# Weights times V summed in one PSUM bank over a group's eight cells, each product placed inside the scores of a later cell

## The chip, the cores and the metric

The kernel runs on one core of a Trainium2 chip. The time is the device time of the whole program in microseconds (us). A profiled execution adds a trace of every instruction on the engines: PE (TensorE, matmuls), DVE (VectorE), ACT (ScalarE), POOL (GpSimd) and SP, which here only issues DMAs. PEld is PE's loading of weights.

## The reference, cut to what matters

Two transformer blocks follow each other, on x of 2 x 1024 tokens of width 256, with 16 heads of 16. Each block has self attention over the 1024 tokens, cross attention over 64 context rows, and a feed-forward part (eight experts with the best two per token in the first block, a plain one in the second). What the change touches is the self attention of both blocks:

```
scores = einsum('bhqd,bhkd->bhqk', q, k) / sqrt(16)
attn = softmax(scores, axis=-1)
out = einsum('bhqk,bhkd->bhqd', attn, v)
```

All of it is in float32.

## The kernel before, in words

`self_attention` runs once for each block. It cuts its work into 128 cells. A cell is one block of 128 keys for one half of the queries (512) and four heads; eight cells in a row are a group (`h`): they share queries and heads, and go through all 1024 keys. Two batches, two halves of the queries and four sets of heads give 16 groups.

For each cell two kinds of scores are made, four tiles of each, one tile for a head:

- kind "b", keys by queries: two matmuls (the queries are kept as a high and a low part) and a third with one-rows that subtracts each query's maximum. ACT turns the tile into weights with exp (L873), written to `pt`.
- kind "a", queries by keys, for the cell that lies `LEAD` = 10 cells ahead: two matmuls, and DVE takes the maximum of each row (L866, `mx`). At a group's end `collect` (L916 to L918) and `largest` (L770, L772) bring the maxima into the form that the third matmul of kind "b" needs.

`scores` (L878) writes these in **waves**. There are four lanes, one for each head and each on 32 rows of the PE array. Lanes 0 and 1 do "b" and then "a", lanes 2 and 3 the other way round. One wave is one matmul of each lane, so a cell has five waves. A tile takes one of PSUM's eight banks: `bank()` pops the head of the list `free`, and the bank goes back to the tail once its drain (ACT or DVE) is written down. PE must wait where a popped bank is still being read. The wave in which a tile begins is therefore the place of such a wait (L894 is the line of all these matmuls).

`product` (L929) multiplies the weights of cells past with V (L938; V carries a column of ones, so that the sums of the weights come with it). It takes a bank from the list, holds it for one or two cells, copies it with ACT (L947 for the first of a group, to `acc`; L950 for the others, to `part`) and adds the part to `acc` (L951, on POOL while maxima are still made, on DVE after that). It is called after the scores, at each even cell for the two cells before, or at an odd cell for one of them when there is little other work (`alone`).

At the end of each cell the loop (L1030 to L1065) hands out other work: a `Stream` of tasks with costs and due times, which are projections of keys and queries (`project_heads`, L646, with ACT L633 and DVE L634), values (L609), the output projection (L440), transposes and norms (L372), cross attention (L1182, L1216, L1269, L1283) and so on. Each step pops its own bank and gives it back. `owed` and `most` say how much is handed out in one cell. Between the two loops lie the experts, and after the second one the last feed-forward part; what the loops leave over is done there.

Engines work in the order in which the program is written; the order on PE, DVE, ACT and SP is set by hand (`manual_schedule`), and only semaphores stand between them.

Of the kernel before, what the change touches and what calls it, by code (L numbers as in the profile page):

```python
# [41 lines left out]
F32 = mybir.dt.float32  # L42
# [4 lines left out]
ALU = mybir.AluOpType  # L47
# [4 lines left out]
P = 128  # L52
# [4 lines left out]
TB = S // P  # L57
# [11 lines left out]
VW = 18  # L69
# [135 lines left out]
def two_blocks(  # L205
# [16 lines left out]
    nc = tc.nc  # L222
# [6 lines left out]
    )  # L229
    banks = psum.tile([P, 8, 512], F32, tag="banks", name="banks")  # L230
    free = list(range(8))

    def bank():


        i = free.pop(0)
        return i, banks[:, i, :]
# [79 lines left out]
    def helper():  # L317

        return nc.gpsimd if maxima[0] else nc.vector
# [175 lines left out]
    def next_heads():  # L495

        npair[0] += 1
        return npair[0] - 1

    def invert(n, sm):  # L500

        nc.vector.reciprocal(sm, sm)
        nc.sync.dma_start(out=turns[n], in_=sm)
# [22 lines left out]
    def self_attention(layer, tail, heads, arrive, extra, when_ready, beside=None):  # L526
# [6 lines left out]
        names = f"s{layer}"  # L533
        pools = ExitStack()

        def results_pool():
            side = {"side": "right"} if layer else {}
            return tail.enter_context(tc.tile_pool(name=f"opool{layer}", bufs=2, **side))
# [4 lines left out]
        if layer == 0:  # L543
            opool = results_pool()
# [13 lines left out]
        stream, later = Stream(RATE[layer]), {}  # L558
        maxima[0] = True

        def at_cell(cell, go):
            later.setdefault(cell, []).append(go)

        extra(stream, vpool, at_cell)
        ncell = 64 * B
        xT, V, ot, sums, acc = {}, {}, {}, {}, {}
        QB, mx = {}, {}
        exps = {}
# [207 lines left out]
        def finish(h, cell):  # L776


            b, qh, g = h // 8, h // 4 % 2, h % 4
            if g == 0:  # L780
                ot[b, qh] = opool.tile([P, 2, 512], F32, tag="ot", name=f"ot_{names}{b}{qh}")
            if layer == 0 and h >= 8 * B - 2:

                if g == 3:
                    stream.add(
                        side_by_side([acc.pop(h - 1), acc.pop(h)], ot[b, qh][:, 1, :]), 2.0,
                        mark="compact", rank=80,
                    )
                    project(b, qh, ["compact"])
                return  # L790
            if g % 2 == 0:
                sm = small.tile([P, 32], F32, tag="sums", name=f"sums_{names}{h}")
                sums[g // 2] = next_heads(), sm
            n, sm = sums[g // 2]
            dst = ot[b, qh][:, g // 2, :]
            send(acc.pop(h), n, g % 2, sm)
            if g % 2 == 1:
                by = opool.tile([P, 512], F32, tag="by", name=f"by_{names}{h}", bufs=1)
                gather(n, dst)
                at_cell(cell + 1, lambda: invert(n, sm))  # L800
                at_cell(cell + 2, lambda: spread_out(n, by))

                late = 3 + maxima[0]
                at_cell(cell + late, lambda: divide(dst, by))
                if g == 3:
                    at_cell(cell + late + 1, lambda: project(b, qh))
# [68 lines left out]

            return products, drain

        def scores(lanes):  # L878

            lanes = [[score(*t) for t in lane] for lane in lanes]  # L880
            at = [[0, None] for _ in lanes]
            while any(lanes):
                done = []
                for lane, now in zip(lanes, at):
                    if not lane:
                        continue
                    products, drain = lane[0]
                    if now[1] is None:
                        now[1] = bank()
                    i, sc = now[1]  # L890
                    lhsT, rhs = products[now[0]]
                    now[0] += 1
                    last = now[0] == len(products)
                    nc.tensor.matmul(sc, lhsT=lhsT, rhs=rhs, start=now[0] == 1, stop=last)  # L894
                    if last:
                        done.append((drain, i, sc))
                        lane.pop(0)
                        now[:] = 0, None
                for drain, i, sc in done:
                    drain(sc)  # L900
                    free.append(i)

        def early(cell):

# [19 lines left out]
                    break  # L924
                most -= cost

        alone = set()

        def product(cells):  # L929

            h = cells[0] // 8
            b, g = h // 8, h % 4
            for cell in cells:
                stream.until(("values", b, cell % 8 & 6))
            n, o = bank()
            for cell in cells:
                for j in range(4):
                    nc.tensor.matmul(  # L938
                        o[32 * j : 32 * j + VW, :],
                        lhsT=V[b][:, cell % 8, 4 * g + j, :],  # L940
                        rhs=exps.pop((cell, j)),
                        start=(cell == cells[0]),
                        stop=(cell == cells[-1]),
                    )
            if cells[0] % 8 == 0:
                acc[h] = opool.tile([P, 512], F32, tag="acc", name=f"acc_{names}{h}")
                nc.scalar.copy(acc[h], o)  # L947
            else:
                part = opool.tile([P, 512], F32, tag="part", name=f"part_{names}{cells[0]}", bufs=3)
                nc.scalar.copy(part, o)  # L950
                helper().tensor_tensor(acc[h], acc[h], part, ALU.add)  # L951
            free.append(n)
            if cells[-1] % 8 == TB - 1:
                at_cell(cells[-1] + 3, lambda: finish(h, cells[-1] + 3))

        def begin():

# [20 lines left out]
        if layer == 0:  # L978
            ws = twice()
            norm_pairs(0, TB, ln, x_turned(0), f"{names}0", arrive)  # L980
            other_constants()
            prepare()
            for i in range(2):
                spread_bias(i)
            for _ in first_heads(ws):
                pass
            ready_for_exp()
            stream.add(biases(), 3.3, last=6, mark="biases")
        else:
            beside(begin)  # L990
            beginning.close()
            stage[0] = mixture.spare
            opool, qpool = results_pool(), weights_pool()
            stream.made.add(("QB", 0))
        stream.made.update([("norm", 0), ("Q", 0)])
        add_values(0, -99, [("norm", 0)])
        add_heads(2)
# [12 lines left out]
        if layer == 0:  # L1010

            fill_up(-LEAD, 4.0)
            owed = 0.0
            for ahead in range(0, LEAD, 2):
                cell = now[0] = ahead - LEAD
# [13 lines left out]
        owed = 0.0  # L1029
        for cell in range(ncell + 2):  # L1030
            now[0] = cell
            ahead = cell + LEAD
            if ahead < ncell and ahead % 16 == 0:
                need_heads(ahead // 8)
            has_a, has_b = ahead < ncell, cell < ncell
            maxima[0] = has_a
            lanes = []
            for j in range(4):
                tiles = [("b", cell, j)] * has_b + [("a", ahead, j)] * has_a
                lanes.append(tiles[::-1] if j > 1 else tiles)  # L1040
            scores(lanes)
            if ahead % 8 == 7 and has_a:
                h = ahead // 8
                collect(h)
                stream.add(largest(h), 0.75, first=cell + 1, last=cell + 2, mark=("QB", h))
            if (cell + 1) % 8 == 0 and cell + 1 < ncell:
                stream.until(("QB", (cell + 1) // 8))
            for go in later.pop(cell, []):
                go()
            owed = min(owed, 3.0) + max(stream.pace(cell), 0.0 if has_a else 2.0)  # L1050
            if cell >= 2 and cell % 2 == 0:
                product([c for c in (cell - 2, cell - 1) if c not in alone])
                if owed < 2.5:
                    continue
            most = 3.0
            while owed > 0.6 and most > 0.0:
                cost = stream.step(cell)
                if cost is None:
                    break
                owed -= cost  # L1060
                most -= cost

            if cell % 2 == 1 and most > 2.0 and cell < ncell:
                alone.add(cell - 1)
                product([cell - 1])  # L1065
        pools.close()
        return stream, later

# [990 lines left out]
    stream, later, _, _ = block(0, tail)  # L2059
# [41 lines left out]
    def beside(begin):  # L2101

        both = Stream(0.0)
        both.add(begin(), 40.0, mark="begun", rank=50)
        both.add(mixture.run(NFIRST, NEVEN), 72.0, mark="slots")
        both.rest({}, 0)
        ready_for_exp()
        mixture.others()
        slots.close()

    with ExitStack() as tail:
        stream, later, made, ready = block(1, tail, heads, beside)
# [157 lines left out]
```

## Time and profile before

| what | us |
|---|---|
| three runs | 1635.91, 1643.36, 1648.19 |
| median | 1643.36 |
| profiled execution, its own time | 1634.33 |
| its span (first to last instruction) | 1632.5 |
| PE busy | 1510.0 (92%) |
| DVE busy | 1056.7 (65%) |
| ACT busy | 940.5 (58%) |
| POOL busy | 459.6 (28%) |
| L866, maxima on DVE, 1024 of 680 ns | 633.0 |
| L873, exp on ACT, 1024 of 605 ns | 532.6 |
| L938, products on PE, 2048 of 639 ns | 280.9 |
| L951, adds on POOL, 149 of 1283 ns | 191.2 |
| L950, part copies on ACT, 163 of 601 ns | 97.9 |

Busy time is the union of an engine's records, so records that overlap count once. A float32 matmul of the source stands in the trace as two (1024 products are 2048 records). A row of the timeline gives start, duration, engine, line and operation, the tile written and the tiles read, how many follow each other, and in brackets how long the engine had been idle and for whom. A row of the waits view says which engine and line waited for which, in total. A row of the windows view gives each engine's busy time in a stretch, then the granted clock of PE as a share of full speed, the DMA share, and GB/s.

### The profile page before, as it was taken

Reading aid. Unit: us, or ns where it says so; the run is one execution under the profiler, and the core shown is the slowest. Engines: PE = TensorE matmul, PEld = TensorE weight load, DVE = VectorE, ACT = ScalarE, POOL = GpSimd, SP = SyncE. Lnnn points to the kernel's source line nnn. Section 1 sums busy time; section 2 is a strip of 40 time slices with the busy share of each in tenths; the row PEclk is TensorE's granted clock in tenths of the full one; section 3 lists DMA queues with packets and bytes.
Section 4 is the critical chain, followed back from the end, with each engine's and each line's share of the span. In section 5 each row is a group of like instructions: output and inputs, shape, how many; then the busy total and the mean of one; then the engine's idle time right before and its main releaser. Section 6 shows DMA issues by size and latency. Waiting matters only on the chain. (4 is left out here: it accounts for less than half of the span.)

```text
span 1632.5 us, 30066 instructions
## 1 busy us (share of the span) xinstructions
PE 1510.0 (92%) x11230; PEld 885.1 (54%) x11230; DVE 1056.7 (65%) x2287; ACT 940.5 (58%) x1820; POOL 459.6 (28%) x584
## 2 busy tenths in 40 slices
PE   7999998988898986999999998999998998989998
PEld 3534544444444454788888764444444444446766
DVE  6798777887887764531114576978788886855400
ACT  3478777856776752423322336876776786774321
POOL 1234333433533302121112023411353344421010
PEclk9799999999998897999999999999999999999999
DMA  4446331201100120666566123111231112000000
GB/s 162 157 157 243 100 107 48 82 34 47 59 28 14 34 81 33 233 241 209 194 204 241 66 95 100 34 60 41 85 105 47 34 53 76 21 8 21 14 13 26
DMA packets 66481, 147.36 MB, mean 90 GB/s; under 512 B 10650, under 2 KB 24860, under 8 KB 65948
## 3 DMA queue, kind: packets, MB, share of 16 engines
q1 hardware_dynamic: 62876, 135.89, 24.3%
q0 software_dynamic: 3456, 9.51, 1.6%
q8 instruction: 90, 1.47, 0.4%
q14 instruction: 59, 0.48, 0.1%
HBM read 92.61 MB, written 52.51 MB: 89 GB/s over the span
## 5 line engine op out<-in xcount | busy, mean ns | idle before, releaser
L866 DVE TENSOR_REDUCE mx_s<-banks 128x1 f32<-128x512 f32 x1024 | 633.0, 680 | 105.8 <-PE banks L894 103.7
L873 ACT ACTIVATE pt_s<-banks 128x512 f32<-128x512 f32 x1024 | 532.6, 605 | 121.8 <-PE banks L894 117.6
L938 PE MATMUL banks<-pt_s,v_s 128*18 128x512 f32 x2048 | 280.9, 639 | 51.4 <-DVE mx_s L866 50.5
L951 POOL TENSOR_TENSOR acc_s<-acc_s,part_s 128x512 f32<-128x512 f32 x149 | 191.2, 1283 | 345.3 <-ACT part_s L950 343.7
L894 PE MATMUL banks<-qb_s,ones 2*128 2x512 f32 x1024 | 207.9, 407 | 0.0
L950 ACT COPY part_s<-banks 128x512 f32<-128x512 f32 x163 | 97.9, 601 | 79.3 <-PE banks L938 47.2
L1799 PE MATMUL banks<-w_slot,h_s 128*128 128x256 f32 x640 | 143.1, 380 | 0.1
L938 PEld LDWEIGHTS banks<-pt_s,v_s 128*18 128x18 f32 x2048 | 43.4, 99 | 180.6 <-DVE mx_s L866 124.1
L1799 PEld LDWEIGHTS banks<-w_slot,h_s 128*128 128x128 f32 x640 | 120.6, 190 | 18.8 <-DVE mx_s L866 1.3
L1808 DVE SCALAR_TENSOR_TENSOR ys<-banks,gate,b 128x256 f32<-128x256 f32 x40 | 19.3, 483 | 154.8 <-PE banks L1799 152.5
L1814 POOL DMA_INDIRECT results<-ys,to x40 | 38.8, 970 | 246.6 <-DVE ys L1808 178.2
L894 PEld LDWEIGHTS banks<-qb_s,ones 2*128 2x128 f32 x1024 | 101.2, 194 | 7.7 <-DVE qb_s L772 0.3
L1775 ACT ACTIVATE h_s<-banks,w_slot 128x256 f32<-128x256 f32 x104 | 43.6, 470 | 105.5 <-issue 64.9
L1769 PE MATMUL banks<-xsT,w_slot 128*128 128x256 f32 x416 | 94.8, 381 | 0.7 <-ACT xsT L379 0.7
L1769 PEld LDWEIGHTS banks<-xsT,w_slot 128*128 128x128 f32 x416 | 77.5, 190 | 12.6 <-ACT xsT L379 1.4
L1932 ACT ACTIVATE h_f<-banks,w_ff 128x512 f32<-128x512 f32 x32 | 22.0, 687 | 73.9 <-PE banks L1929 73.9
L1775 ACT ACTIVATE h_s<-banks,spare 128x256 f32<-128x256 f32 x56 | 23.5, 470 | 61.3 <-issue 30.4
L1237 POOL TENSOR_TENSOR sc_c<-sc_c,mx_c 128x512 f32<-128x512 f32 x36 | 37.6, 1045 | 73.2 <-DVE mx_c L1236 73.1
L1941 PE MATMUL banks<-w_ff,h_f 128*128 128x256 f32 x256 | 57.3, 380 | 0.0
L1929 PE MATMUL banks<-hT_f,w_ff 128*128 128x512 f32 x128 | 56.4, 593 | 0.0
L1216 PE MATMUL banks<-kbd,q_c 32*128 32x128 f32 x512 | 48.5, 293 | 4.5 <-DVE mx_s L866 2.9
L1941 PEld LDWEIGHTS banks<-w_ff,h_f 128*128 128x128 f32 x256 | 48.0, 190 | 7.8 <-issue 1.4
(362 smaller groups left out, 3216.2 us busy)
## 6 DMA issues: line engine op xcount, KB each, us to landing
w_slot<-in_ff_w_dram SPq DMA_DIRECT2D x40, 576.0 KB
sorted_rows<-fill SPq DMA_DIRECT2D x36, 520.0 KB
w_slot<-in_ff_w_dram SPq DMA_DIRECT2D x26, 514.0 KB
whole<-acc_s SPq DMA_DIRECT2D x30, 256.0 KB
spare<-in_ff_w_dram SPq DMA_DIRECT2D x14, 514.0 KB
q_parts<-spare SPq DMA_DIRECT2D x14, 512.0 KB
k_parts<-spare SPq DMA_DIRECT2D x12, 512.0 KB
KS<-k_parts SPq DMA_DIRECT2D x12, 512.0 KB
```

The lines of the kernel that those rows point to most:

```text
L866: return products, lambda sc: nc.vector.tensor_reduce(to, sc, AX.X, ALU.max)
L873: nc.scalar.activation(pt, sc, AF.Exp, scale=SCALE)
L894: nc.tensor.matmul(sc, lhsT=lhsT, rhs=rhs, start=now[0] == 1, stop=last)
L938: nc.tensor.matmul(o[32 * j : 32 * j + VW, :], lhsT=V[b][:, cell % 8, 4 * g + j, :], rhs=exps.pop((cell, j)), start=(cell == cells[0]), st ...
L950: nc.scalar.copy(part, o)
L951: helper().tensor_tensor(acc[h], acc[h], part, ALU.add)
L1216: nc.tensor.matmul(p[:, t * P : (t + 1) * P], lhsT=q[rows, g, t * P : (t + 1) * P], rhs=kbd[rows, g, b].rearrange("p u k -> p (u k)"), sta ...
L1769: nc.tensor.matmul(ph[:, n, :], lhsT=w[:, at : at + P], rhs=xT[:, k, :], start=(k == 0), stop=(k == 1),)
L1775: nc.scalar.activation(h1[:, f, :], ph[:, n, :], AF.Gelu, bias=w[:, W_B1 + f : W_B1 + f + 1])
L1799: nc.tensor.matmul(py, lhsT=h1[:, f, h * P : (h + 1) * P], rhs=w[:, f * D : (f + 1) * D], start=(f == 0), stop=(f == 7),)
L1929: nc.tensor.matmul(ph, lhsT=w1[:, at : at + P], rhs=hT[:, k, :], start=(k == 0), stop=(k == 1))
L1941: nc.tensor.matmul(py[:, n, :], lhsT=h1[:, f, t * P : (t + 1) * P], rhs=w2[:, f * D : (f + 1) * D], start=(f == 0), stop=(f == 7),)
```

## The change

Bank 7 (`SUMS`) is taken out of the list for the length of each loop, and seven banks remain in turn. `product` now does one cell. It adds into bank 7 over all eight cells of a group: the first starts the sum, the eighth ends it, and one ACT copy takes it to `acc`. The parts and their adds are gone. `scores` calls `product(cell - 2)` between its third wave and its fourth. Banks that the scores have emptied no longer go back one by one: those of the first three waves go back together after the third, and those of the last two at the end, taken alternately from the two halves. The rules of how much other work a cell gets lose the case of even cells, and `most` falls from 3.0 to 1.8.

```diff
+    SUMS = 7
...
-        def scores(lanes):
+        def scores(lanes, beside=None):
             lanes = [[score(*t) for t in lane] for lane in lanes]
             at = [[0, None] for _ in lanes]
+            emptied, wave = [], 0
             while any(lanes):
...
                 for drain, i, sc in done:
                     drain(sc)
-                    free.append(i)
+                emptied.extend(i for _, i, _ in done)
+                wave += 1
+                if wave == 3 or not any(lanes):
+                    half = (len(emptied) + 1) // 2
+                    for n in range(half):
+                        free.extend(emptied[n::half])
+                    emptied = []
+                if wave == 3 and beside:
+                    beside()
...
-        def product(cells):
+        def product(cell):
+            h, n = divmod(cell, 8)
             b, g = h // 8, h % 4
-            for cell in cells:
-                stream.until(("values", b, cell % 8 & 6))
-            n, o = bank()
-            for cell in cells:
-                for j in range(4):
-                    nc.tensor.matmul(
-                        o[32 * j : 32 * j + VW, :],
-                        lhsT=V[b][:, cell % 8, 4 * g + j, :],
-                        rhs=exps.pop((cell, j)),
-                        start=(cell == cells[0]),
-                        stop=(cell == cells[-1]),
-                    )
-            if cells[0] % 8 == 0:
+            stream.until(("values", b, n & 6))
+            o = banks[:, SUMS, :]
+            for j in range(4):
+                nc.tensor.matmul(
+                    o[32 * j : 32 * j + VW, :],
+                    lhsT=V[b][:, n, 4 * g + j, :],
+                    rhs=exps.pop((cell, j)),
+                    start=(n == 0),
+                    stop=(n == TB - 1),
+                )
+            if n == TB - 1:
                 acc[h] = opool.tile([P, 512], F32, tag="acc", name=f"acc_{names}{h}")
                 nc.scalar.copy(acc[h], o)
-            else:
-                part = opool.tile([P, 512], F32, tag="part", name=f"part_{names}{cells[0]}", bufs=3)
-                nc.scalar.copy(part, o)
-                helper().tensor_tensor(acc[h], acc[h], part, ALU.add)
-            free.append(n)
-            if cells[-1] % 8 == TB - 1:
-                at_cell(cells[-1] + 3, lambda: finish(h, cells[-1] + 3))
+                at_cell(cell + 3, lambda: finish(h, cell + 3))
...
+        free.remove(SUMS)
...
-            scores(lanes)
+            if has_b:
+                scores(lanes, (lambda: product(cell - 2)) if cell >= 2 else None)
+            else:
+                product(cell - 2)
...
-            if cell >= 2 and cell % 2 == 0:
-                product([c for c in (cell - 2, cell - 1) if c not in alone])
-                if owed < 2.5:
-                    continue
-            most = 3.0
+            most = 1.8
             while owed > 0.6 and most > 0.0:
...
-            if cell % 2 == 1 and most > 2.0 and cell < ncell:
-                alone.add(cell - 1)
-                product([cell - 1])
+        free.append(SUMS)
```

More of the change, by code (lines that the diff above doesn't have):

```diff
@@ L925, in fill_up @@
                 most -= cost
-        alone = set()
-        def product(cells):
-            h = cells[0] // 8
+        def product(cell):
+            h, n = divmod(cell, 8)
             b, g = h // 8, h % 4
-            for cell in cells:
-                stream.until(("values", b, cell % 8 & 6))
-            n, o = bank()
-            for cell in cells:
-                for j in range(4):
-                    nc.tensor.matmul(
-                        o[32 * j : 32 * j + VW, :],
-                        lhsT=V[b][:, cell % 8, 4 * g + j, :],
-                        rhs=exps.pop((cell, j)),
-                        start=(cell == cells[0]),
-                        stop=(cell == cells[-1]),
-                    )
-            if cells[0] % 8 == 0:
+            stream.until(("values", b, n & 6))
[9 more added lines that the diff above has]
+            if n == TB - 1:
                 acc[h] = opool.tile([P, 512], F32, tag="acc", name=f"acc_{names}{h}")
                 nc.scalar.copy(acc[h], o)
-            else:
-                part = opool.tile([P, 512], F32, tag="part", name=f"part_{names}{cells[0]}", bufs=3)
-                nc.scalar.copy(part, o)
-                helper().tensor_tensor(acc[h], acc[h], part, ALU.add)
-            free.append(n)
-            if cells[-1] % 8 == TB - 1:
-                at_cell(cells[-1] + 3, lambda: finish(h, cells[-1] + 3))
+                at_cell(cell + 3, lambda: finish(h, cell + 3))
         def begin():
```

## Prediction

> **What bounds the kernel now.** I read the busy shares first, then the windows of the two attention loops, then the waits, then one stretch of the timeline.
>
> The page says PE 92%. That share is inflated, because a matmul's record lasts longer than the array needs it (0.39 to 0.49 us for one that frees the array after 0.23). What tells more is the pair of windows over the two loops of 128 cells each:
>
> ```profile
> core 0: us, PE busy (x) PEld busy (x) DVE busy (x) ACT busy (x) POOL busy (x), PEclk, DMA share, GB/s
> 47.50:574.80 527.30, 482.67 (x4166) 233.93 (x4166) 425.37 (x840) 380.20 (x736) 197.56 (x249) 0.94 0.25 86
> 964.40:1468.80 504.40, 464.27 (x4138) 223.50 (x4140) 387.06 (x722) 371.15 (x710) 182.00 (x210) 0.96 0.18 60
> ```
>
> The loops take 527.3 + 504.4 = 1031.7 us, or 4.06 us a cell for 254 cells (the first of each counts to the start). DVE works 3.2 us of that and ACT 3.0. No engine is full: the cell is a chain between engines. The waits name its links:
>
> ```profile
> engine line waited for: us in total, times, longest us
> POOL acc_s L951 <- ACT part_s L950: 343.7, 89, 17.3
> ...
> PEld banks L894 <- DVE mx_s L866: 137.4, 235, 1.7
> PEld banks L938 <- DVE mx_s L866: 124.1, 174, 4.2
> ...
> PE banks L938 <- DVE mx_s L866: 50.5, 66, 3.8
> ```
>
> Scores (L894) and products (L938) wait for DVE's maxima (L866), since each needs a bank that DVE is still reading. POOL waits for its parts, so its adds are off the path. The timeline shows one cell that has no other work:
>
> ```profile
> 128.51 1.05 PE L938 MATMUL banks<-pt_s,v_s 128*18 128x512 f32 x8
> ...
> 129.50 0.50 PE L894 MATMUL banks<-QS02h,KS 32*128 32x512 f32 x2
> ...
> 129.83 0.40 PE L894 MATMUL banks<-QS02l,KS 32*128 32x512 f32 x2
> ...
> 130.06 0.39 PE L894 MATMUL banks<-qb_s,ones 2*128 2x512 f32 x2
> ...
> 130.87 0.40 PE L894 MATMUL banks<-qb_s,ones 2*128 2x512 f32 x2
> ...
> 131.20 0.62 PE L938 MATMUL banks<-pt_s,v_s 128*18 128x512 f32 x4
> ```
>
> Starts, read downward: product, 0.99 us to the first wave of scores, 0.33 to the second, 0.23 to the third, 0.81 to the fifth, 0.33 to the next product. The period is 2.69. DVE's four reductions take 2.47 in a row (1132.79, x4), 0.60 from one to the next, each 0.68 until its bank is free. So DVE is nearly full in this cell. The product lies just where PE would else wait: the fifth wave's maximum needs 0.39 (matmul) + 0.04 + 0.68 (L866) + 0.05 (release to PE) = 1.16 us until its bank is free, and the product fills 0.33 + 0.98 = 1.31 of that.
>
> By this pattern a cell costs max(2.65, 2.44 + s) us, s being PE time of other tasks at its end; 0.10 of it is the switch to such a task and is paid only where there is one. Over the 254 cells that gives 903 us. The real 1032 hold 129 us of excess: products that stall for a DVE bank, DVE stretched by POOL's adds, and half clock after the stalls.
>
> **What goes.** 163 part copies on ACT (97.9 us) and 163 adds (149 on POOL, 191.2 us; 14 on DVE). Neither engine bounds a cell, so this alone saves only what the adds do to DVE:
>
> ```profile
> 110.67 1.28 POOL L951 TENSOR_TENSOR acc_s<-acc_s,part_s 128x512 f32<-128x512 f32 x1 [1.63 <-ACT part_s L950]
> 110.77 1.22 DVE L917 CAST spread<-top_s 128x16 fp32r<-128x16 f32 x1
> ...
> 113.40 1.19 PE L938 MATMUL banks<-pt_s,v_s 128*18 128x512 f32 x8 [1.86 <-DVE mx_s L866]
> ```
>
> The cast takes 0.18 us elsewhere and 1.22 beside the add; behind it the maxima come late, and the product waits 1.86 us. Summed over the loops, DVE rows that outlast their usual time lose 20 us. The product's bank wait goes too: bank 7 is its own. What is late next is the score wave, below.
>
> **What moves.** I read the order of the new program: first three waves, product, last two waves, then the other tasks. With seven banks, the fourth score of wave one waits for DVE, and so does the fourth of wave three, the second of wave four and the second of wave one. The product itself waits for nothing. Following the free list by hand: wave one's fourth score takes the bank of the previous cell's third maximum (call it a0), wave three's fourth takes that of the last maximum (a1), wave four's second takes this cell's first.
>
> Chain of a cell without other work, from the start of a0's reduction: a1 starts at 0.60, ends at 1.28, PE is released at 1.33 (wave one's release at 0.73, plus 0.34 and 0.25 for two waves, gives 1.32, the same). Product at 1.66. Wave four at 1.66 + 0.98 = 2.64. Its bank is free since 1.20 + 0.68 = 1.88, so no wait. Wave five at 2.97, done at 3.36, next a0 at 3.40 to 3.41. **The period is 3.41 instead of 2.65.** The product now stands on the chain, and the 1.16 us behind wave five, which it used to fill, are open for other tasks: up to 0.84 us of them cost nothing. A cell with more is bound by PE: 0.33 + 0.23 + 0.33 + 0.98 + 0.33 + 0.33 = 2.57 with the switch, plus s.
>
> The order lists what follows each cell. Priced by PE blocks of the trace (one projection of heads L646 1.8 us, L609 and half of L440 1.8, L770 0.5, a block of L1216 1.7, L1269 0.9, plus 0.1 for each visit), 141 of 254 cells have at most 0.84 us, 104 of them nothing; 113 have more, 245 us together.
>
> - 141 x 3.41 = 481
> - 113 x 2.57 + 245 = 536
> - sum 1017, against 1032 measured before
>
> So the new ideal is nearly the old reality. What decides is how much excess comes on top. DVE has 3.41 - 2.47 = 0.9 us free in a plain cell, which hides most of its small work (0.6 of statistics, 0.65 of collecting), and the product stalls are gone, so I expect far less than 129:
> - 23 projections of heads: DVE's second half (L634) starts after PE and ACT (0.69) and ends some 1.75 us after the block; the maximum behind it frees its bank at 2.5, wave four wanted it at 1.9: 0.6 each, 14 us
> - two banks taken by small tasks: wave one waits for a1, 0.57 each, some 7 cells: 4 us
> - clock (next part): 20 us
> - the 3 us wait of the second layer's keys for a DMA, and DVE lumps over 0.9: 12 us
>
> Together 50. The copy of the finished sum (32 of 0.6 us on ACT) must end before the next group's first product, more than 2 us later: nothing, and if that cover failed, 0.6 each, 19 us. The sending of a finished sum (`finish`) stays three cells behind its last cell; that cell's product now comes half a cell later and its add no longer follows, so SP's stores find it ready as before. Other tasks take at most 1.8 us a cell instead of 3.0; by the order 7.6 us of PE work (258.6 against 251.0) moves behind the loops, where PE is full (40.00 of 40.00 us in the last whole slices): +8. No DMA is added; those of finish, keys and queries keep their cells, give or take one.
>
> Sum: 1017 + 50 + 8 - 1032 = **+43 us**. Bounds: excess 0 gives -7, the old 129 gives +122.
>
> **A rule against the row.** The Trainium skill, TensorEngine Tiling (Array Packing), Key Properties, says that changing the tiling mode drains the array. Scores use four row tiles, products four column tiles, so each product inside the scores is two changes more wherever other tasks follow. By the row a change costs about 0.1 us: 0.33 against 0.23 from wave to product, 0.98 for a product alone against 0.92 in a pair (1.84 to the next start for x16). By the rule taken at its word, each side exposes the whole tail of a matmul, 0.39 in place of 0.1; the plain cell would be 3.41 + 0.58 = 4.0 and the kernel 150 us slower. I take the row, as the same two changes stand in it; it already speaks against the change by 0.2 a cell.
>
> The page TensorE: Matmul & The Clock Gate, Part 1, says that the clock halves after an idle window of about 3.4 us. Here it halves sooner:
>
> ```profile
> 114.20:117.60 3.40, 3.40 (x28) 2.22 (x24) 2.83 (x7) 0.88 (x2) 1.27 (x1) 0.50 0.01 2
> ```
>
> That follows the 1.86 us stall above. By the rule a plain cell never throttles (idle 0.5 us at a time): no cost. By the trace, waves at half clock step 0.42 and a cell loses some 1.1 us, and of 23 windows of 3.4 us at full clock in which the matmuls stood as thin as they will in the new plain cell, 4 were followed by half clock: 141 x 0.17 x 1.1 = 26, at most. Between 0 and 26 I take 20, nearer to the row.
>
> **Rivals.**
> *Clock.* Spread waits halve the clock in a third or more of the plain stretches, half of it again feeding back through longer cells: 141 x 0.5 x 1.1 = 78 in place of 20, sum +100, **1740**. For it: PE is really at work only 72% of a plain cell. Against: no wait is long.
> *Excess gone.* The slack swallows nearly all of it: excess 0 to 15, so -7 to +8, **1640**. For it: most stalls in the waits view belong to L938. Against: projections still chain PE, ACT and DVE.
> *Cheap switches (faster).* Place: the product inside the scores. If the switch costs nothing once no semaphore holds the product, waves stay 0.23 apart and the product costs 0.87; the plain cell is 1.33 + 0.23 + 0.87 + 0.23 + 0.43 = 3.10, others lose 0.23 each: 1017 - 44 - 26 = 947, +58 - 1032 = -27, **1612**. It decides from about 3.1 us a plain cell. For it: a pair of products is cheaper per cell. Against: 0.33 appears after every switch, waiting or not.
> *Not what it says.* If the compiler's order had the product wait for the sum's copy each cell, PE would lose 0.6 us x 254 = 152, **1790**; the order shows no such wait, so it gets no chance of its own.
>
> **Numbers.** The profiled run took 1634.33 us (span 1632.5), 9 below the median 1643.36 and just below the lowest timed run. The sum gives 1677 on the profiled run and 1686 on the median; I give 1682, and the rivals on the same middle (1639). Chances: forecast (1660 to 1710) 0.50, clock 0.20, excess gone 0.14, cheap switches 0.16. About 1% (1627 to 1660) is what can be told from no change. Range 1618 to 1760: low is near the cheap switches, high beyond the clock case.
>
> **What would show it.** Right: in plain cells scores restart every 3.4 us; PE waits for DVE sit before waves one and three, none before the product; the adds are gone and L917 is 0.18; the loops together take about 1075. Wrong: a plain period near 2.7 to 3.1, or the first waves waiting for nothing, or loops at or below 1020.

## The result and the profile after

The changed kernel takes **1691.3 us** (median of four, 1686.2 to 1700.0), against 1639.6 us (four, 1631.8 to 1648.2) for the kernel before on the same chip: a ratio of **1.032, 95% interval 1.025 to 1.039**, slower. The profiled execution took 1694.1 us, with a span of 1692.3 against 1632.5, so 59.8 us are to be explained in the traces (8 more than the 51.7 between the medians: the profiled execution before was one of the shorter ones, the one after one of the longer). The page's busy row of the changed kernel:

```profile
PE 1572.9 (93%) x11230; PEld 877.3 (52%) x11230; DVE 1048.6 (62%) x2275; ACT 871.2 (51%) x1655; POOL 268.1 (16%) x433
```

POOL lost 191 us and ACT 69: the adds and part copies are gone, and the kernel is slower all the same. PE does the same 11230 matmuls, and the durations of their records add up to nearly the same (5146 us against 5131). They are spread out and overlap less, so the time that at least one of them covers is 63 us longer: "busy" is not work here.

The windows over the two loops, with the same marks as in the prediction (the first and last numbers of a row are the stretch, then its length, then each engine's busy time):

```profile
core 0: us, PE busy (x) PEld busy (x) DVE busy (x) ACT busy (x) POOL busy (x), PEclk, DMA share, GB/s
50.10:606.10 556.00, 516.17 (x4136) 227.70 (x4138) 412.10 (x822) 342.16 (x647) 96.64 (x169) 0.93 0.23 80
1015.00:1529.60 514.60, 481.59 (x4120) 213.84 (x4114) 385.92 (x713) 333.98 (x626) 86.40 (x134) 0.98 0.16 55
```

The loops take 1070.6 us in place of 1031.7. By stretches, from the starts of the matmul records:

| stretch | before | after | difference |
|---|---|---|---|
| before the second cell of loop one | 62.9 | 65.5 | +2.6 |
| loop one, from its second cell to its last | 511.9 | 540.7 | +28.8 |
| from there to the second cell of loop two | 394.7 | 406.2 | +11.5 |
| loop two, the same | 499.3 | 509.5 | +10.2 |
| from there to the end of the last matmul | 159.3 | 166.0 | +6.7 |

So 39 us lie inside the loops and 18 behind them. The waits of the changed kernel:

```profile
ACT pt_s L875 <- PE banks L898: 326.4, 391, 6.3
PEld banks L898 <- DVE mx_s L868: 212.8, 385, 1.9
...
DVE mx_s L868 <- PE banks L898: 173.0, 231, 3.0
...
PEld banks L898 <- ACT pt_s L875: 165.2, 194, 1.7
...
PEld banks L946 <- issue: 77.8, 254, 0.7
...
PE banks L898 <- DVE mx_s L868: 61.6, 125, 1.6
```

The products (L946 now) wait for DVE nowhere: the 174.6 us that L938 waited are gone. But the scores' waits for DVE grew from 137 to 213 on the loads, with 62 more on the matmuls, and now ACT and DVE stand idle for PE (326 and 173 us, against 118 and 104 before). Every engine waits for another: the cell has become a longer chain. The row with ACT as releaser is a trap: the load before wave four is idle while the eight matmuls of the product run, and ACT's release is only the last event before it.

The timeline of one cell without other work, a plain cell (start, duration, engine and line):

```profile
150.04 1.05 PE L946 MATMUL banks<-pt_s,v_s 128*18 128x512 f32 x8
...
151.03 0.50 PE L898 MATMUL banks<-KS,QS03h 32*128 32x512 f32 x2
...
151.37 0.40 PE L898 MATMUL banks<-KS,QS03l 32*128 32x512 f32 x2
...
151.79 2.59 DVE L868 TENSOR_REDUCE mx_s<-banks 128x1 f32<-128x512 f32 x4 [0.83 <-PE banks L898]
...
152.54 0.49 PE L898 MATMUL banks<-KS,QS03h 32*128 32x512 f32 x1 [0.54 <-DVE mx_s L868]
...
152.88 0.40 PE L898 MATMUL banks<-qb_s,ones 2*128 2x512 f32 x2
...
153.13 0.18 PEld L898 LDWEIGHTS banks<-QS02h,KS 32*128 32x128 f32 x1 [0.29 <-DVE mx_s L868]
...
153.56 1.05 PE L946 MATMUL banks<-pt_s,v_s 128*18 128x512 f32 x8
...
154.54 0.18 PEld L898 LDWEIGHTS banks<-KS,QS03h 32*128 32x128 f32 x2 [0.85 <-ACT pt_s L875]
```

Read down the starts: product, 0.99 to wave four, 0.34 to wave five, 0.42 until DVE begins its four maxima, 0.75 until the first of them has released wave one's fourth score, 0.34 to wave two, 0.25 to wave three, whose last score waited for DVE, 0.43 to the next product. The period is 3.52 us, where it was 2.69. DVE is idle for 0.83 of it, waiting for wave five, and wave five waits for the product.

### The profile page after: what moved, and what is told of

It is laid out like the page before. It is cut to its first block, busy times and chain, and to the rows that moved or that the text cites. A ratio compares the mean times of both kernels' runs of the same rounds, so it can differ in the third digit from the quotient of the medians.

```text
span 1692.3 us, 29474 instructions
## 1 busy us (share of the span) xinstructions
PE 1572.9 (93%) x11230; PEld 877.3 (52%) x11230; DVE 1048.6 (62%) x2275; ACT 871.2 (51%) x1655; POOL 268.1 (16%) x433
## 5 line engine op out<-in xcount | busy, mean ns | idle before, releaser
L868 DVE TENSOR_REDUCE mx_s<-banks 128x1 f32<-128x512 f32 x1024 | 654.5, 683 | 176.8 <-PE banks L898 173.0
L875 ACT ACTIVATE pt_s<-banks 128x512 f32<-128x512 f32 x1024 | 555.4, 599 | 338.8 <-PE banks L898 326.4
L946 PE MATMUL banks<-pt_s,v_s 128*18 128x512 f32 x2048 | 283.3, 627 | 0.0
L946 PEld LDWEIGHTS banks<-pt_s,v_s 128*18 128x18 f32 x2048 | 34.9, 97 | 78.9 <-issue 77.8
L898 PE MATMUL banks<-KS,QS00h 32*128 32x512 f32 x128 | 45.4, 505 | 11.4 <-DVE mx_s L868 11.0
L648 PE MATMUL banks<-xT_s,w_att 128*128 128x512 f32 x104 | 53.8, 645 | 0.6 <-ACT pt_s L875 0.6
L898 PE MATMUL banks<-KS,QS12h 32*128 32x512 f32 x128 | 43.5, 508 | 11.6 <-DVE mx_s L868 9.3
```

The costliest lines, as they stand in the source:

```text
L648: nc.tensor.matmul(p, lhsT=w[:, at + k * D + pair * P : at + k * D + (pair + 1) * P], rhs=xT[b][:, k, blk * 512 : (blk + 1) * 512], start= ...
L868: return products, lambda sc: nc.vector.tensor_reduce(to, sc, AX.X, ALU.max)
L875: nc.scalar.activation(pt, sc, AF.Exp, scale=SCALE)
L946: nc.tensor.matmul(o[32 * j : 32 * j + VW, :], lhsT=V[b][:, n, 4 * g + j, :], rhs=exps.pop((cell, j)), start=(n == 0), stop=(n == TB - 1),)
```

## The experiments

All ratios are to the kernel before on the same chip (medians 1636 to 1640). The last column is the length of a plain cell at full clock with one product: the median, and in brackets the 10th and the 90th percentile. Where the product stands inside the scores, it is taken from wave four to the next wave four, else from wave one to wave one.

| run | banks in turn | product | us | ratio, 95% interval | plain cell, us |
|---|---|---|---|---|---|
| kernel before | 8 | after the scores | 1640 | 1 | 2.77 (2.51 to 3.45) |
| changed kernel | 7 | inside | 1691 | 1.032 (1.025 to 1.039) | 3.52 (3.51 to 3.69) |
| inside_with_parts | 8 | inside | 1683 | 1.027 (1.023 to 1.031) | 3.52 (3.51 to 3.67) |
| sum_outside_pairs | 7 | after | 1759 | 1.072 (1.068 to 1.077) | 3.18 (3.17 to 3.73) |
| sum_outside_each | 7 | after | 1745 | 1.068 (1.062 to 1.074) | 3.18 (3.17 to 3.88) |
| inside_most3 | 7 | inside | 1680 | 1.024 (1.020 to 1.029) | 3.52 (3.51 to 3.70) |
| half_product_inside | 7 | inside | 1683 | 1.024 (1.016 to 1.031) | 3.10 (3.08 to 3.48) |
| half_product_outside | 8 | after | 1594 | 0.974 (0.970 to 0.977) | 2.63 (2.21 to 3.48) |
| half_maxima_inside | 7 | inside | 1606 | 0.981 (0.977 to 0.985) | 3.12 (3.11 to 3.22) |
| half_maxima_outside | 8 | after | 1570 | 0.957 (0.952 to 0.962) | 2.68 (2.46 to 3.29) |
| outside_act_bank | 8 | after | 1623 | 0.991 (0.988 to 0.994) | 2.89 (2.69 to 3.63) |
| half_maxima_act_bank | 8 | after | 1557 | 0.952 (0.949 to 0.955) | 2.68 (2.68 to 3.14) |

So the changed kernel has one chain that nearly every plain cell follows, while a plain cell before had no single length: it was often longer than the 2.65 that the forecast priced.

### The sum's bank without the new place, and the place without the sum's bank

**sum_outside_pairs**: the kernel before, its sum kept in bank 7, its products where they were.

```diff
-            n, o = bank()
+            o = banks[:, SUMS, :]
...
-                        start=(cell == cells[0]),
-                        stop=(cell == cells[-1]),
+                        start=(cell % 8 == 0),
+                        stop=(cell % 8 == TB - 1),
...
-            if cells[0] % 8 == 0:
+            if cells[-1] % 8 == TB - 1:
...
-            else:
-                part = opool.tile([P, 512], F32, tag="part", name=f"part_{names}{cells[0]}", bufs=3)
-                nc.scalar.copy(part, o)
-                helper().tensor_tensor(acc[h], acc[h], part, ALU.add)
-            free.append(n)
...
+        free.remove(SUMS)
```

> The sum in bank 7 alone: products stay after the scores, at the old places and by the old rules. Theory A (the place of the product costs the time, 3.52 us for a cell without other work against 2.65): at or below the kernel before, 1600 to 1640 us. Theory B (the bank that the sums take is what costs): with seven banks the second score of wave four must take the bank of this cell's first maximum, free only 1.5 us after wave one; with no product to hide it, every cell loses about 0.5 us: a cell without other work 3.1, others 3.0 + s, loops 1027 + 30 to 80, so 1670 to 1720 us.

Measured: 1758.6 us, the slowest of all, although copies and adds are gone. The timeline of a plain cell shows where:

```profile
197.42 0.50 PE L896 MATMUL banks<-QS00h,KS 32*128 32x512 f32 x2
...
198.20 2.59 DVE L868 TENSOR_REDUCE mx_s<-banks 128x1 f32<-128x512 f32 x4 [0.32 <-PE banks L896]
...
198.95 0.49 PE L896 MATMUL banks<-KS,QS01h 32*128 32x512 f32 x1 [0.32 <-DVE mx_s L868]
...
199.28 0.39 PE L896 MATMUL banks<-qb_s,ones 2*128 2x512 f32 x2
...
199.61 1.05 PE L940 MATMUL banks<-pt_s,v_s 128*18 128x512 f32 x8
...
200.59 0.50 PE L896 MATMUL banks<-QS00h,KS 32*128 32x512 f32 x2
```

With one bank less, a score of wave four needs the bank of this cell's own first maximum, so the scores wait for DVE in the middle of a cell and the product is added behind: 0.78 + 0.75 + 0.33 + 0.33 + 0.98 = 3.17 us.

**sum_outside_each**: the changed kernel with the product called after the scores.

```diff
             if has_b:
-                scores(lanes, (lambda: product(cell - 2)) if cell >= 2 else None)
-            else:
+                scores(lanes)
+            if cell >= 2:
                 product(cell - 2)
```

> The changed kernel with the product of each cell right after its scores instead of inside. Theory A: about 1640 us, cells without other work at 2.7. Theory B: the wait before wave four shows in each cell, cells without other work 3.1 and others 3.0 + s, so no faster than the changed kernel, 1680 to 1730 us.

Measured: 1745.1 us, the same plain cell of 3.18. Cells with one projection of 1.8 us of PE work mostly take 5.09, against 4.47 in the changed kernel: there too the wave-four wait stands open.

**inside_with_parts**: the changed kernel with eight banks in turn, each emptied bank returned at once, and the parts copied and added as before, one for each cell.

```diff
-                emptied.extend(i for _, i, _ in done)
+                    free.append(i)
...
-            o = banks[:, SUMS, :]
+            n, o = bank()
...
+            else:
+                part = opool.tile([P, 512], F32, tag="part", name=f"part_{names}{cells[0]}", bufs=3)
+                nc.scalar.copy(part, o)
+                helper().tensor_tensor(acc[h], acc[h], part, ALU.add)
+            free.append(n)
...
-        free.remove(SUMS)
```

> The place alone: products inside the scores, but each with its own bank out of eight, its part copy and its add. Theory A: cells without other work 3.5, 1680 to 1710 us. Theory B: no bank is missing, so about the time before, 1640 us.

Measured: 1683.2 us, plain cell 3.52. The products follow each other at that distance with eight banks too:

```profile
130.90 1.05 PE L942 MATMUL banks<-pt_s,v_s 128*18 128x512 f32 x8
...
134.42 1.05 PE L942 MATMUL banks<-pt_s,v_s 128*18 128x512 f32 x8
...
137.94 1.05 PE L942 MATMUL banks<-pt_s,v_s 128*18 128x512 f32 x8
...
141.46 1.05 PE L942 MATMUL banks<-pt_s,v_s 128*18 128x512 f32 x8
```

These kernels answer the main question. With eight banks the new place costs 44 us. Keeping the sum in a bank costs 106 to 120 us with the product after the scores, although copies and adds go with it. With the product inside, where it lies just in front of wave four and covers its wait, it costs 8 us, less than the two intervals can tell apart. So the place is what makes the lost bank bearable, and it is also what costs the time. Two things come with the place here. One is the lower `most`, which the next run parts from it in the changed kernel; eight banks with the old limit were not run. The other is a product, a copy and an add for each cell in place of many pairs. The alternating order in which the changed kernel returns its banks has no run of its own either; the plain cell is 3.52 with it and without it.

### The work that is handed out

**inside_most3**: the changed kernel with the old limit.

```diff
-            most = 1.8
+            most = 3.0
```

> The changed kernel with up to 3.0 us of other work in a cell instead of 1.8. Theory A: work bunches, more cells stand without any and pay 3.52, 1690 to 1705 us. Rival (the work that 1.8 pushes behind the loops): 7.6 us back, 1680 us.

Measured: 1679.7 us, 12 below the changed kernel, with intervals that overlap a little. In the traces the loops take 6 us more (524.0 + 531.9 against 540.7 + 509.5), but the stretches behind them are back at 397.0 and 157.6, within 3 us of before. So the lower limit is nearly all of the 18 us behind the loops, and buys a third of that inside them.

### Shorter products

**half_product_inside** and **half_product_outside**: each product over 256 of its 512 queries, in the changed kernel and in the kernel before.

```diff
-                    o[32 * j : 32 * j + VW, :],
+                    o[32 * j : 32 * j + VW, :256],
...
-                    rhs=exps.pop((cell, j)),
+                    rhs=exps.pop((cell, j))[:, :256],
```

> The changed kernel with products over 256 of the 512 queries only (the other half of the result repeats the first), 0.43 us less of PE a cell. Theory A (the product stands on the chain of every cell): cells without other work 3.52 - 0.43 = 3.09, all 254 cells shorter, -109 us, 1585 us. Rival (the waits for DVE's maxima set the 3.52 whatever the product takes): only the cells bound by PE gain, 113 x 0.43 = -48, 1643 us.

> The same halving in the kernel before (the part copies write the first half twice). Theory A (after the scores the product fills a hole, so its length matters only where PE bounds the cell): cells without other work stay at 2.6, -45 us, 1595 us. Rival: as much as inside, -109, 1530 us.

Measured: outside 1594.0, as forecast, though partly by luck: half clock in its two loops rose to 207 us from 102, which the forecast did not count. Inside 1682.7, some 100 us above the forecast, and only 9 below the full product. The plain cell did fall to 3.10 wherever the clock was full. But for 365 us of the two loops the clock was halved (91 in the changed kernel; all four figures from the second cell of each loop to its last). At half clock a plain cell took 4.56. A window of half_product_inside, then the same stretch of half_product_outside, columns as above:

```profile
core 0: us, PE busy (x) PEld busy (x) DVE busy (x) ACT busy (x) POOL busy (x), PEclk, DMA share, GB/s
110.50:150.00 39.50, 37.05 (x248) 16.00 (x247) 24.88 (x48) 19.14 (x36) 2.85 (x14) 0.50 0.31 111
```

```profile
110.50:150.00 39.50, 35.96 (x355) 16.44 (x355) 35.37 (x65) 31.42 (x61) 18.01 (x26) 0.91 0.48 174
```

The granted clock is 0.50 throughout, while PE's records leave hardly a gap (37.05 of 39.50), and it does 248 matmuls where the other does 355. The four executions ranged from 1662 to 1697 us and the profiled one is the longest. But the mean clock of the other three was 0.893 to 0.913 too, where the four of the changed kernel had 0.954 to 0.966; even the shortest lies 77 above the forecast. The step that failed in this expectation is the clock, not the chain.

### Shorter maxima

**half_maxima_inside** and **half_maxima_outside**: DVE takes each maximum over 256 of the 512 keys.

```diff
-                return products, lambda sc: nc.vector.tensor_reduce(to, sc, AX.X, ALU.max)
+                return products, lambda sc: nc.vector.tensor_reduce(to, sc[:, :256], AX.X, ALU.max)
```

> The changed kernel with DVE's maxima over 256 of 512 keys only, some 0.27 us less each. Theory A (release of the maxima, then three waves, product, two waves are one chain): cells without other work about 3.25, others as before, 140 x 0.27 = -38, 1653 us. Rival (PE alone is the bound): no change, 1690 us.

> The kernel before with each cell's maxima over 256 of the 512 keys of a score instead of all (which only shifts the softmax), the product and its banks left where they were: the partner of half_maxima_inside. Place theory (what the change costs is the place of the product; DVE bounds the plain cell before and no longer does here): a plain cell falls from 2.65 to about 2.45 us, now bound by the scores, the product and the waits between them; 113 cells with work change little; 1590 to 1610, at or below half_maxima_inside's 1606. Rival (with shorter maxima the place no longer matters, since inside gained 86 us by them and outside has only 0.2 us a plain cell to gain): above 1615, so that the inside order would be the better one once DVE is short.

Measured: 1605.8 inside, 47 below the expectation; 1569.9 outside, 20 below the lower end of its band. Inside, the plain cell is 3.12 in place of the expected 3.25: the release of wave one comes 0.28 sooner, and wave three no longer waits alone, which takes 0.10 off the step to the product (0.33 in place of 0.43). The further 0.13 of a plain cell is 18 us over 140 cells, and half clock in the loops fell from 91 to 46 us, worth some 16 by the two lengths of a plain cell in the changed kernel (5.41 at half clock, 3.52), an estimate; the rest of the 47 is open. DVE is thus two links of the new chain, not its bound. Outside, the median of a plain cell falls from 2.77 to 2.68. The place, with the bank and the limit that come with it, still costs 36 us; of the 33 by which the two profiled spans differ, 19 lie inside the loops, 13 behind them, where the work kept back by `most` lies, and 1 ahead. So the rival, that the inside order would win once DVE is short, is out. The waits of half_maxima_outside say why even the old order gained 66 us:

```profile
DVE mx_s L866 <- PE banks L894: 233.0, 213, 5.6
...
PEld banks L938 <- DVE mx_s L866: 73.3, 153, 3.7
...
PE banks L938 <- DVE mx_s L866: 14.4, 15, 3.3
```

The products' waits for DVE halve, from 174.6 to 87.7, and DVE now waits 233 us for PE, 104 before.

### Another way to take away the products' waits

**outside_act_bank**: the kernel before, with one rule more. The product takes the first free bank that DVE did not drain last.

```diff
+    slow = set()
...
+        slow.discard(i)
...
                 for drain, i, sc in done:
                     drain(sc)
                     free.append(i)
+                    if drain.__name__ != "drain":
+                        slow.add(i)
...
-            n, o = bank()
+            n = next((i for i in free if i not in slow), free[0])
+            free.remove(n)
+            slow.discard(n)
+            o = banks[:, n, :]
```

> The kernel before, but each product takes the first free bank that ACT drained last, instead of the head of the list, which DVE is often still reading. Theory (the excess of the kernel before is products stalled behind late maxima, 50 us of dead PE at L938): most of that comes back, 1600 to 1620 us. Rival (the stall only moves to the next wave of scores, which needs the same maximum): 1635 to 1640 us.

Measured: 1623.5 us over eight executions, 0.991 (0.988 to 0.994), a few us above the expected band, and the fastest of the kernels that do all of the work. Its waits:

```profile
PEld banks L896 <- DVE mx_s L868: 167.4, 299, 2.1
...
PEld banks L945 <- ACT pt_s L875: 81.1, 182, 0.8
...
ACT part_s L957 <- PE banks L945: 36.1, 47, 2.2
```

The products (L945) have no row of waits for DVE any more; ACT's 81 us are 0.45 for each of 182 loads, of which the 0.33 from the last wave to a product would pass anyway. The scores wait 30 us more for DVE. The plain cell is no shorter (median 2.89, against 2.77); the gain is in the cells with other work, and half clock in the loops fell from 102 to 58 us. (The profiled execution is the shortest of the eight, so it shows the rule at its best.) So the 175 us for which products waited on DVE can be taken away without moving the product; of the time, 16 us came back, and how much of that is the clock is not shown.

**half_maxima_act_bank**: the same with the shorter maxima.

> outside_act_bank with maxima over 256 of the 512 keys. If what that rule of banks gained (16 us) was a wait of the product for a bank that DVE drains late, shorter maxima make DVE drain in time, and it is within 6 us of half_maxima_outside. If the gain came from the order of the banks in the next cell's scores, it is again about 15 us below half_maxima_outside, 1575 to 1595.

Measured: 1557.4 us (1552.6 to 1559.8), 12.5 below half_maxima_outside (1557.4 to 1572.7), with intervals of the ratios that overlap. That is nearer to the theory of the banks' order than to that of the late drain, but does not settle it: half clock in the loops is 34 us against 61, and the plain cell has the same median (2.68) with the shorter cells gone.

## Why the prediction was right, and where it was not

The measured 1691 lies 9 above the forecast and inside the likeliest case's own range of 1660 to 1710.

**Plain cell: right in kind, 0.11 us short.** Forecast 3.41, measured 3.51 to 3.53. All links but one are within 0.02 us of the sum: release 0.75, waves 0.34 and 0.25, product to wave four 0.99, wave five 0.34, to the next maximum 0.42. The link that was mis-sized is wave three to product, priced at 0.33 from a wave that does not wait and measured at 0.43. Wave three's last score starts alone after its wait for DVE. Its record lasts 0.49 in place of 0.39, and the product starts later by the same 0.10. half_maxima_inside, in which it does not wait, shows 0.39 and 0.33. For the forecast's 141 cells, 0.11 each is 15 us.

**Other cells: right.** Forecast 2.57 + s; with one projection of 1.8 us and a switch 4.47, measured 4.46 to 4.50 in 11 of 15 at full clock, up to 5.21 in the rest. And small work is free behind wave five, as forecast: of 10 cells with one block of `largest` (L772) alone, seven take 3.52 or 3.53.

**The rule and the row.** The Trainium skill's rule that a change of tiling mode drains the array (TensorEngine Tiling (Array Packing), Key Properties), taken at its word, would have made the plain cell 4.0; the row made it 3.41. The measured 3.52 decides for the row, with the one addition above.

**Where the waits are: right.** PE's waits for DVE sit before waves one and three, none before a product. The cast that took 1.22 us beside an add is short again, and the maxima follow it at once:

```profile
156.84 0.18 DVE L929 CAST spread<-top_s 128x16 fp32r<-128x16 f32 x1
157.06 0.19 DVE L930 TENSOR_TENSOR spread<-top_s,spread 128x16 f32<-128x16 f32 x1
157.16 1.28 DVE L868 TENSOR_REDUCE mx_s<-banks 128x1 f32<-128x512 f32 x2
```

**The sum of the loops: near, partly by luck.** Forecast +35 (1017 + 50 - 1032; its 536 is 535 by its own terms), so 1067 (the 1075 that it names as a sign counts the 8 us behind the loops in), measured 1071, +39. Over the 252 cells from the second of each loop on, the ideal by the forecast's own prices, an estimate, can be set beside the measured time: before 859 and 1011, after 974 and 1050. The step that failed is the ideal over 254 cells: for the two first cells it counted 43 us, work that is handed out ahead of the loops included, while the 1032 held 21 for them. That put 22 us too much into 1017. It was made up by 15 us too little for the plain cells and 10 too little excess (60 beyond the right plain cell, forecast 50). By the same prices the excess of before was 152, not 129, and 92 of it went. A part of it lay in the plain cells themselves (median 2.77, priced at 2.65).

**Clock: the amount near, the price of a cell too low.** Half clock in the loops is 91 us after, 102 before. A plain cell at half clock takes 5.41, so it loses 1.9 us and not 1.1: the 91 us, as some 17 such cells at 1.9, are 32 us, an estimate, where 20 were set aside. half_product_inside shows that the clock rival was a real danger: chains hardly thinner than this one fell into half clock for 61 us at a time.

**Behind the loops: 18 us, forecast 8.** The forecast counted 7.6 us of PE work that moves there at its own length. inside_most3 brings back nearly all of it with the limit of 3.0, so the limit is the cause; it costs over twice the PE time that it moves. A part of the rest may be the clock, which the forecast put at nothing here. Between the loops it was halved for 34 us, against 20 before and 24 in inside_most3 (27 to 34 in the five kernels with the limit of 1.8, 20 to 31 in the others). Waves step 0.42 at half clock and 0.23 at full, so 14 us more of it can cost up to some 6, an estimate. Behind the second loop the clock shows no such difference (3 us after, 5 in inside_most3), and the rest is open.

**The rivals.** Excess gone did not come: 60 us stayed. Cheap switches is out: waves beside a product stay 0.34 apart and the plain cell is not 3.1. The sum's copy holds no product: L946 waited for it twice, 0.7 us in all.

## What to carry to other kernels

Before an operation is moved, ask what it covers where it stands. The product filled the 1.16 us in which wave five's maximum freed its bank; its new place opened that gap and put 0.98 us on the chain between two waves, for +44 us with all eight banks (the lower limit and the products one by one included). A buffer taken out of a rotation is priced by following the free list for one cell, not by the engines' shares: giving one bank to the sum cost over 100 us in one order and 8 in the other. And when the largest waits are those for a slow drain, try first whether the waiter can take a buffer that another engine drains: that gave 0.9% for a few lines, far less than the waits it took away, since others took their place (81 us for ACT, and 30 more for DVE before the scores).

## What was not expected of the hardware

- The clock stayed halved though no long idle stretch shows. In half_product_inside it was 0.50 for 61.4 us twice; between 110.5 and 150.0 us the longest gap between matmul records was 0.35 us (a record can outlast the step to the next wave, 0.39 against 0.23 at full clock, so the array's own gaps may be longer). The rule of an idle window of about 3.4 us (the Trainium skill, TensorE: Matmul & The Clock Gate, Part 1), which gave the prediction's low end for the clock, does not by itself explain a half clock that holds through such gaps. In the same stretch half_product_outside had 0.91. What sets it was not settled; the run shows that a shorter matmul can give back nearly all that it saves.
- A score that starts alone after a wait holds up the next product by 0.10 us more than one that did not wait (0.43 from start to start against 0.33), and its record is longer by as much (0.49 against 0.39).
- A wait of 0.85 us on the weight load put down to ACT, in each plain cell, costs nothing: the next wave starts 0.99 after the product, as it did before (0.99) with DVE named.
